# Starting the first row's score maxima beside the second row's input stage

## The chip, the cores and the metric

The kernel runs on one core of one Trainium2 chip. The metric is the device time of one execution in microseconds (us). The kernel before was timed three times: 1706.95, 1707.77 and 1711.70 us, so the median is 1707.77 us. A profile was taken of one further execution.

## The reference, cut to what matters

The input x has 16 rows (b = 0 to 15) of 512 tokens with 128 features. Six residual blocks follow each other. Each begins with a layer norm.

```
x = x + 0.5 * kan(norm(x))          # small two-layer net per feature ("kan" below)
x = x + attention(norm(x))          # 16 query heads, 4 key heads, head size 8, rope, causal softmax
x = x + 0.5 * kan(norm(x))
x = x + 0.5 * experts(norm(x))      # 8 experts, each takes its 128 best tokens of every row
x = x + recurrence(norm(x))
x = x + 0.5 * experts(norm(x))
```

Only the first two blocks matter for the change. In the attention block, the scores of a query with all keys up to it are turned into weights by a softmax: the largest score of each query and head is subtracted before the exponential. So for each row the kernel first finds the maxima of the scores and then computes the scores a second time, with the maxima taken off, for the exponential.

## The kernel before, in words

**Layout.** A row is one tile of 128 partitions x 4 x 128 numbers. The kernel treats the 16 rows one after another through a pipeline of stages, and the stages of different rows lie beside each other. All engine orders (TensorE, VectorE, ScalarE, GpSimd) are the order in which the program emits the instructions; each engine works strictly through its own list. The SP engine, which issues the DMAs, also works through one list.

**Stages of a row.** `stage_in` (L582) runs `kan` (L329) and then `attn_in` (L415). `attn_in` normalizes the row, makes queries, keys and values with matrix products (L424, L430, L436, L444), applies rope on VectorE (L425, L431, L437, L445), and splits queries and keys into three bf16 parts on ScalarE and GpSimd (`parts`, L393, eight GpSimd operations with the rope sums at L440 and L463). `spread` (L408) then writes the parts to DRAM, and the packed keys `kp` (three DMAs, L476) and packed queries `qp` (four DMAs, one for each key head r, L484) are read back. There are NKP = 3 buffers of packed keys, so row b uses the buffer of row b - 3, and NQP = 10 buffers of packed queries.

`maxima` (L597) finds the row's score maxima in 44 steps, 11 for each of the four key heads: a step is a score product on TensorE (L611, with a causal mask added by L607 where a bank holds several heads) and one reduction on VectorE (L616 or L621). Two PSUM banks take turns, so TensorE can be at most two steps ahead of VectorE. After each half, `max_rows` (L625) turns the maxima into rows and sends them by DMA (L649, L651) into the packed queries.

`weights` (L657) computes the scores again in 44 steps: product on TensorE (L669), exponential on ScalarE (L672), mask on GpSimd (L674). It sets `taken[0]` to the number of key heads that have been emitted so far, over all rows. `outputs` (L680) multiplies by the values, and `stage_out` (L718) closes the attention, runs the second `kan` and the gate of the experts.

**The order is a matter of turns.** Everything is a Python generator; a *turn* (`turn`, L1098) emits what was put off (`flush`), gives one step to every urgent and every side generator and refills a budget for each engine. The main loop (L1127) goes over b from -1 to 15. A pass lasts TURNS = 44 turns, and in each turn one step of `weights(b)` and one step of `maxima(b + 1)` are emitted. The pass b = -1 has only the maxima of row 0, and the pass b = 0 is the first with weights. From b = 0 on the side generators are held to the engine budgets (`paced`). `forward` (L576) runs the `kan` of later rows ahead as long as `filling` is set, which is until the pass b = 0 begins.

**The start.** The pass b = -1 begins only when `finish(first, second)` (L1124) has run turns until the input stages of rows 0 and 1 are both completely emitted. Followed through the program's own counters, this gives the following turns for the kernel before:

| emitted | turn |
|---|---|
| row 0: DMAs of `kp` and `qp` | 45 |
| row 1: `attn_in` begins / its DMAs of `kp` and `qp` | 49 / 70 |
| pass b = -1 begins (maxima of row 0) | 71 |
| row 2: `attn_in` begins / its DMAs | 72 / 93 |
| `kan` of row 3 | 67 to 98 |
| `kan` of row 4 | 98 to 129 |
| pass b = 0 begins (weights of row 0, maxima of row 1) | 115 |
| row 3: `attn_in` begins / its DMAs | 138 / 165 |
| pass b = 1 begins | 159 |
| pass b = 2 begins | 203 |

At the end of the passes b = 0 and later `finish(ins[b + 2])` (L1157) makes sure that the row needed two passes later is through.

Of the kernel before, what the change touches and what calls it, by code (L numbers as in the profile page):

```python
# [25 lines left out]
NR = 4  # L26
# [3 lines left out]
NKP = 3  # L30
# [16 lines left out]
def tile_macaron(  # L47
# [10 lines left out]
    B = x_in.shape[0]  # L58
# [40 lines left out]
    with ExitStack() as ph:  # L99
# [90 lines left out]
        def packed(b):  # L190
            return [QP[(NR * b + r) % NQP] for r in range(NR)], KP[b % NKP]
# [17 lines left out]
        def step(g):  # L209
            return g is not None and next(g, g) is not g  # L210
# [10 lines left out]
        def need(**work):  # L221
            while paced[0] and any(w > room[e] for e, w in work.items()):
                yield
            for e, w in work.items():
                room[e] -= w

        def take(**work):

            for e, w in work.items():
                room[e] -= w  # L230

        def refill():
            now[0] += 1
            room.update(MOST)
# [8 lines left out]
        def bank(shape, dtype, name, work=0.0):  # L243


            while held[0] == 2 or (paced[0] and work > room["pe"]):
                yield
            room["pe"] -= work
            held[0] += 1
            return mm.tile(shape, dtype, name=name, tag="mm")  # L250

        def freed():
            held[0] -= 1
# [154 lines left out]
        def spread(part, heads, name):  # L408

            scr = tc.dram_tile([3, HD, heads, S], BF16, name=name)  # L410
            for i in range(3):
                nc.sync.dma_start(out=scr[i].rearrange("d h t -> h d t"), in_=part[:, i, :])
            return scr

        def attn_in(b, st):  # L415
            _, xT = yield from norm(x[b])
            ka = w1p.tile([KR, S], F32, name="rope_ka")
            kb = w1p.tile([KR, S], F32, name="rope_kb")
            ta = w1p.tile([P, S], F32, name="rope_a")
            tb = w1p.tile([P, S], F32, name="rope_b")  # L420
            qpart = w1p.tile([P, 3, S], BF16, name="qpart")
            kpart = w1p.tile([KR, 3, S], BF16, name="kpart")
            pa = yield from bank([P, S], F32, "ps_pa", 0.9)
            nc.tensor.matmul(pa, lhsT=wq.rearrange("k h d -> k (h d)"), rhs=xT, start=True, stop=True)  # L424
            later.append(lambda: nc.vector.tensor_mul(ta, pa, rope[:, 0, :]))  # L425
            yield
            take(dve=0.7)
            freed()
            pb = yield from bank([P, S], F32, "ps_pb", 0.9)
            nc.tensor.matmul(pb, lhsT=wqr.rearrange("k h d -> k (h d)"), rhs=xT, start=True, stop=True)  # L430
            later.append(lambda: nc.vector.tensor_mul(tb, pb, rope[:, 1, :]))  # L431
            yield
            take(dve=0.7)
            freed()
            pk = yield from bank([2 * KR, S], F32, "ps_pk", 0.9)
            nc.tensor.matmul(pk, lhsT=wk.rearrange("k w h d -> k (w h d)"), rhs=xT, start=True, stop=True)  # L436
            later.append(lambda: nc.vector.tensor_mul(ka, pk[0:KR, :], rope[0:KR, 0, :]))  # L437
            yield
            yield from need(pool=1.25)
            nc.gpsimd.tensor_tensor(ta, ta, tb, ALU.add)  # L440
            take(dve=0.7)
            pv = yield from bank([P, NT, KR], F32, "ps_v", 0.9)
            for c in range(NT):
                nc.tensor.matmul(pv[:, c, :], lhsT=xT[:, bass.ts(c, P)], rhs=wv, start=True, stop=True)  # L444
            later.append(lambda: nc.vector.tensor_mul(kb, pk[KR : 2 * KR, :], rope[KR : 2 * KR, 1, :]))  # L445
            yield
            take(dve=0.7)
            freed()
            qp_steps = parts(ta, qpart, nc.scalar.copy, act=0.6)
            step(qp_steps)  # L450

            va = vap.tile([P, NT, NR, 32], F32, name="va")
            nc.gpsimd.memset(va[:, :, :, HD:32], 0.0)
            nc.gpsimd.memset(va[:, :, :, HD : HD + 1], 1.0)
            later.append(lambda: nc.vector.tensor_copy(va[:, :, :, 0:HD], pv.rearrange("p c (r d) -> p c r d", d=HD)))
            yield
            take(dve=0.3)
            freed()
            st["va"] = va

            def keys():
                yield from need(pool=1.25)
                nc.gpsimd.tensor_tensor(ka, ka, kb, ALU.add)  # L463
                yield
                yield
                yield
                yield from parts(ka, kpart, nc.scalar.copy, act=0.6)

            yield from together(qp_steps, keys())
            qp, kp = packed(b)  # L470

            ks = spread(kpart, NR, f"ks{b}")
            qs = spread(qpart, NH, f"qs{b}")
            N = 3 * HD
            for j in range(3):
                nc.sync.dma_start(  # L476
                    out=kp[j * N : (j + 1) * N, :, :],
                    in_=ks[j].rearrange("d r t -> d (r t)").unsqueeze(0).to_broadcast([3, HD, NR * S]),
                )
            for r in range(NR):  # L480
                while taken[0] < NR * b + r - NQP + 1:
                    yield
                src = qs[:, :, r * NG : (r + 1) * NG, :].rearrange("i d h t -> (i d) (h t)")
                nc.sync.dma_start(out=qp[r][0 : 3 * N, :, :],  # L484
                                  in_=src.unsqueeze(0).to_broadcast([3, N, NG * S]))
            yield
# [95 lines left out]
        def stage_in(b, st):  # L582
            late = b in through
            yield from kan_in(b)
            for _ in range(LATE if late and b > 2 else 0):
                yield
            yield from attn_in(b, st)
# [164 lines left out]
        def routing(k, g):  # L752


            while scored[k] < (g + 1) * GB:
                yield
            N = GB * E
            sc3 = scores[g].rearrange("p c b e -> p (c b) e")
            mx = rtp.tile([P, NT * GB], F32, name="mx")
            probs = rtp.tile([P, NT, N], F32, name="probs")  # L760
            pr3 = probs.rearrange("p c (b e) -> p (c b) e", e=E)
# [13 lines left out]
            yield from rest(2)  # L775
            ps = yield from bank([N, NT, P], F32, "ps_p")
            for c in range(NT):
# [314 lines left out]
        taken = [0]  # L1092
        sts = [dict() for _ in range(B)]
# [4 lines left out]
        def turn():  # L1098
            flush()
            urgent[:] = [g for g in urgent if step(g)]  # L1100
            sides[:] = [g for g in sides if step(g)]
            refill()

        def finish(*gs):
            pace, paced[0] = paced[0], False
            while any(g in sides for g in gs):
                turn()
            paced[0] = pace
# [4 lines left out]
        first = stage_in(0, sts[0])  # L1113
# [7 lines left out]
        second = stage_in(1, sts[1])  # L1121
        sides.append(second)
        sides.append(forward())
        finish(first, second)  # L1124
        ins = {2: stage_in(2, sts[2])}
        sides.append(ins[2])
        for b in range(-1, B):  # L1127
            if b == 2:
                sides.append(folded())
                sides.extend(routing(k, g) for k in range(2) for g in range(NG2))  # L1130
            if b == B - 1:
                expert_weights()
                sides.append(fetch())
            filling[0], paced[0] = b < 0, b >= 0
            wts = weights(b, sts[b]) if b >= 0 else None
            mxs = maxima(b + 1, sts[b + 1]) if b + 1 < B else None
            if b >= 0:
                sts[b]["y"] = w2p.tile([P, NT, NR, NG, HD], F32, name="y")
                sts[b]["out"] = []
            for i in range(TURNS):  # L1140
                flush()
                step(wts)
                step(mxs)
                if b >= 0 and i and i % len(BANKS) == 0:
                    urgent.append(outputs(b, sts[b], i // len(BANKS) - 1))
                if b > 0 and i == OUT:
                    sides.append(stage_out(b - 1, sts[b - 1]))
                if b + 4 < B and i == IN:
                    ins[b + 4] = stage_in(b + 4, sts[b + 4])
                    sides.append(ins[b + 4])  # L1150
                turn()
            flush()
            step(mxs)
            if b >= 0:
                urgent.append(outputs(b, sts[b], NR - 1))
            if b >= 0 and b + 2 < B:
                finish(ins[b + 2])  # L1157
        hurry[0], paced[0] = True, False
        while len(sts[B - 1]["out"]) < NR:
# [64 lines left out]
```

## Time and profile before

| quantity | value |
|---|---|
| median of three runs | 1707.77 us |
| the profiled execution's own time | 1714.79 us |
| its span, first to last instruction | 1713.1 us |
| mean granted TensorE clock | 0.965 |
| busy share: TensorE, VectorE, ScalarE, GpSimd | 93%, 66%, 58%, 59% |
| first VectorE reduction of row 0's maxima | 76.3 us |
| first exponential of rows 0, 1, 2, 3 and 4 | 121.3, 164.7, 214.4, 272.2, 326.0 us |

The profile gives, for one execution, when each engine was busy. A pass of the main loop can be read from the trace by the first exponential of each row: row 0's marks the start of the pass b = 0, row 1's that of b = 1, and so on. In the middle of the kernel a pass lasts 53.9 us. "PEclk" and "granted clock" are the share of the full TensorE clock that the chip granted: 1.00 is full, 0.50 half.

### The profile page before, as it was taken

Reading aid. Unit: us, or ns where it says so; the run is one execution under the profiler, and the core shown is the slowest. Engines: PE = TensorE matmul, PEld = TensorE weight load, DVE = VectorE, ACT = ScalarE, POOL = GpSimd, SP = SyncE. Lnnn points to the kernel's source line nnn. Section 1 sums busy time; section 2 is a strip of 40 time slices with the busy share of each in tenths; the row PEclk is TensorE's granted clock in tenths of the full one; section 3 lists DMA queues with packets and bytes.
Section 4 is the critical chain, followed back from the end, with each engine's and each line's share of the span. In section 5 each row is a group of like instructions: output and inputs, shape, how many; then the busy total and the mean of one; then the engine's idle time right before and its main releaser. Section 6 shows DMA issues by size and latency. Waiting matters only on the chain. (4 is left out here: it accounts for less than half of the span.)

```text
span 1713.1 us, 35403 instructions
## 1 busy us (share of the span) xinstructions
PE 1593.3 (93%) x12943; PEld 1106.1 (65%) x12943; DVE 1124.4 (66%) x3606; ACT 1000.5 (58%) x2000; POOL 1019.0 (59%) x1486
## 2 busy tenths in 40 slices
PE   5689999999999999999998898999999999999997
PEld 2234444445454444445444598888888789999997
DVE  6578778888898888898984239444377344762222
ACT  3336767788777876777666663444452334445443
POOL 2635547556665656556636666666672867657773
PEclk9769989999999999999999899999998999999999
DMA  4210111011111111111122122332331323323333
GB/s 121 67 60 27 55 48 41 32 43 52 56 33 39 42 55 34 37 42 55 55 72 59 33 55 58 64 62 62 68 63 39 65 58 75 65 52 72 74 75 49
DMA packets 103093, 94.87 MB, mean 55 GB/s; under 512 B 13197, under 2 KB 91478, under 8 KB 102678
## 3 DMA queue, kind: packets, MB, share of 16 engines
q1 hardware_dynamic: 76060, 67.65, 13.0%
q0 software_dynamic: 26048, 24.93, 9.1%
q8 instruction: 102, 1.67, 0.4%
q14 instruction: 73, 0.60, 0.1%
q10 hardware_dynamic: 810, 0.02, 0.0%
HBM read 59.00 MB, written 37.49 MB: 56 GB/s over the span
## 5 line engine op out<-in xcount | busy, mean ns | idle before, releaser
L674 POOL TENSOR_SCALAR_AFFINE_SELECT pt<-pt 128x128 f32<-128x128 f32 (+2 forms) x704 | 251.7, 364 | 333.2 <-ACT pt L672 328.2
L672 ACT ACTIVATE pt<-ps_st 128x512 f32<-128x512 f32 (+1 forms) x704 | 378.6, 563 | 100.6 <-PE ps_st L669 94.7
L616 DVE CUSTOM_DVE_ANT_0 below<-ps_sc,causal 128x512 bf16<-128x512 f32 (+1 forms) x512 | 315.0, 615 | 81.1 <-PE ps_sc L611 65.7
L933 ACT ACTIVATE mo<-ps_h 128x512 f32<-128x512 f32 x256 | 152.8, 597 | 272.2 <-PE ps_h L931 270.3
L857 POOL DMA_INDIRECT xg<-xnd,tokI x256 | 249.5, 975 | 82.7 <-issue 38.7
L931 PE MATMUL ps_h<-xin,mw 128*128 128x128 f32 x2048 | 281.1, 281 | 0.0
L669 PE MATMUL ps_st<-qp,kp 99*128 99x512 bf16 (+3 forms) x1024 | 258.2, 304 | 21.5 <-ACT pt L672 20.7
L946 PE MATMUL ps_y<-mw,mo 128*128 128x128 f32 x2048 | 275.3, 278 | 2.0 <-DVE mo L955 2.0
L611 PE MATMUL ps_sc<-kp,qp 72*128 72x512 bf16 (+3 forms) x1024 | 261.2, 307 | 11.5 <-DVE maxs L616 6.6
L931 PEld LDWEIGHTS ps_h<-xin,mw 128*128 128x128 f32 x2048 | 252.5, 194 | 6.3 <-issue 3.7
L978 POOL DMA_INDIRECT sum<-ye,tokI x124 | 200.3, 1616 | 94.4 <-issue 38.1
L946 PEld LDWEIGHTS ps_y<-mw,mo 128*128 128x128 f32 x2048 | 252.6, 194 | 4.5 <-DVE mo L955 3.3
L669 PEld LDWEIGHTS <-kp 99*128 99x128 bf16 x1024 | 95.2, 101 | 182.2 <-issue 164.8
L371 ACT ACTIVATE kan_h<-kan_s,rbias,kw 128x512 f32<-128x512 f32 x256 | 205.6, 812 | 4.1 <-PE ps_kg L365 4.1
L692 PE MATMUL ps_av<-pt,va 128*32 128x512 f32 (+3 forms) x2048 | 165.7, 442 | 0.0
L621 DVE TENSOR_REDUCE maxs<-ps_sc 128x2 f32<-128x512 f32 (+1 forms) x192 | 130.1, 685 | 38.4 <-PE ps_sc L611 37.9
L611 PEld LDWEIGHTS <-qp 72*128 72x128 bf16 x1024 | 96.6, 100 | 80.3 <-issue 57.7
L952 DVE TENSOR_TENSOR mo<-mo 128x128 bf16<-128x128 f32 x132 | 38.2, 289 | 131.7 <-ACT mo L937 131.5
L964 PE MATMUL acc<-mo 128*128 128x128 bf16 x1584 | 113.0, 220 | 6.2 <-DVE mo L952 6.1
L692 PEld LDWEIGHTS ps_av<-pt,va 128*32 128x32 f32 x2048 | 53.7, 109 | 94.9 <-issue 43.7
L964 PEld LDWEIGHTS <-mo 128*128 128x128 bf16 x1584 | 99.6, 99 | 23.7 <-issue 22.4
L294 POOL TENSOR_TENSOR ln_rstd<-ln_rstd,mhalf 128x4 f32<-128x4 f32 x96 | 101.7, 1059 | 8.0
(197 smaller groups left out, 2376.9 us busy)
## 6 DMA issues: line engine op xcount, KB each, us to landing
qp<-qs SPq DMA_DIRECT2D x64, 288.0 KB
xnd<-kan_x SPq DMA_DIRECT2D x32, 256.0 KB
sum<-x SPq DMA_DIRECT2D x31, 256.0 KB
qs<-qpart SPq DMA_DIRECT2D x48, 128.0 KB
kp<-ks SPq DMA_DIRECT2D x48, 96.0 KB
x<-in_L_attn_x_dram SPq DMA_DIRECT2D x16, 256.0 KB
mw<-in_L_ffn_w_dram SPq DMA_DIRECT2D x16, 256.0 KB
xg<-xnd,tokI POOLq DMA_INDIRECT x256
```

The source lines that it names most:

```text
L371: nc.scalar.activation(h, sk[half], AF.Relu, bias=rbias[:, half, v : v + 1], scale=kw1[:, half, v : v + 1])
L611: nc.tensor.matmul(v[:, u, 0:n], lhsT=qp[r][0 : 9 * HD, g, bass.ts(c, P)], rhs=kp[0 : 9 * HD, r, 0:n], start=alone, stop=(u == len(gs) - 1 ...
L616: nc.vector.tensor_tensor_reduce(below[:, 0:n], v[:, 0, 0:n], causal[:, S - n : S], 1.0, LOWEST, ALU.add, ALU.max, accum_out=maxs[:, c, h ...
L669: nc.tensor.matmul(v[:, u, 0:n], lhsT=kp[ROWS, r, bass.ts(c, P)], rhs=qp[r][ROWS, g, c * P : S], start=True, stop=True)
L672: nc.scalar.activation(o, v[:, :, 0:n], AF.Exp, scale=HD ** -0.5)
L674: nc.gpsimd.affine_select(out=dg, in_=dg, compare_op=ALU.is_ge, fill=0.0, base=0, pattern=[[0, len(gs)], [1, P]], channel_multiplier=-1)
L692: nc.tensor.matmul(po[32 * g : 32 * g + 32, c * P : S], lhsT=va[:, c, r, :], rhs=pt[:, g, OFF[c] : OFF[c] + n], start=(c == 0), stop=(c == ...
L857: nc.gpsimd.indirect_dma_start(out=xgs[i // E % 2][:, i % E, :], out_offset=None, in_=xnd[b], in_offset=bass.IndirectOffsetOnAxis(ap=tokI[ ...
L931: nc.tensor.matmul(pst[:, f, :], lhsT=mw1[e][:, bass.ts(f, P)], rhs=xins[i // E % 2][:, i % E, :], start=True, stop=True)
L946: nc.tensor.matmul(py, lhsT=hs[u][:, f, :], rhs=mw2[e][:, f, :], start=(f == 0), stop=(f == NF - 1))
L964: nc.tensor.matmul(acc[:, c, :], lhsT=sels[u][:, bass.ts(c, P)], rhs=yes[u][:, w, :], start=(e == 0 and c == 0 and w == 0), stop=(e == las ...
L978: nc.gpsimd.indirect_dma_start(out=sums[k, b], out_offset=bass.IndirectOffsetOnAxis(ap=tokI[g][:, n : n + 1], axis=0), in_=ye[:, b % 2 * ( ...
```

## The change

The input stage of row 1 is no longer waited for. After row 0's input stage has been emitted, nine more turns are run, and then the pass b = -1 begins, while row 1's input stage still runs as a side generator. Row 2's input stage is started there too, as before. Row 1's stage now has to be through by the end of the pass b = -1, for which `finish(ins[b + 2])` is also called at b = -1. Since row 3's input stage can now come early enough to reach its key DMAs before row 0's weights are emitted, `attn_in` waits, before its three key DMAs, until all weights of the row three in front (the last user of the same key buffer) have been emitted.

```diff
@@ attn_in
             ks = spread(kpart, NR, f"ks{b}")
             qs = spread(qpart, NH, f"qs{b}")
             N = 3 * HD
+            while taken[0] < NR * (b - NKP + 1):
+                yield
             for j in range(3):
                 nc.sync.dma_start(
                     out=kp[j * N : (j + 1) * N, :, :],
@@ main part
         second = stage_in(1, sts[1])
         sides.append(second)
         sides.append(forward())
-        finish(first, second)
-        ins = {2: stage_in(2, sts[2])}
+        finish(first)
+
+        for _ in range(9):
+            turn()
+        ins = {1: second, 2: stage_in(2, sts[2])}
         sides.append(ins[2])
         for b in range(-1, B):
             if b == 2:
@@ end of a pass
             step(mxs)
             if b >= 0:
                 urgent.append(outputs(b, sts[b], NR - 1))
-            if b >= 0 and b + 2 < B:
+            if b + 2 < B:
                 finish(ins[b + 2])
```

The same turns for the changed kernel: row 1's `attn_in` still begins at 49 and its DMAs still go out at 70; the pass b = -1 begins at 55; row 2's `attn_in` at 67 and its DMAs at 88; the `kan` of rows 3 and 4 stay at 67 to 98 and 98 to 129; the pass b = 0 begins at 99; row 3's `attn_in` at 98, with its parts written at 126 and its `kp` and `qp` DMAs held until 143; the pass b = 1 begins at 143 and the pass b = 2 at 187. From the pass b = 2 on the instructions of every engine stand in the same order as before, 16 turns earlier: of about 9,410 rows of TensorE's order the last 8,939 are the same.

## The prediction

> **What bounds the kernel now.** I read the page's slices first, since the change touches only the first tenth of the kernel:
>
> ```profile
> PE   5689999999999999999998898999999999999997
> DVE  6578778888898888898984239444377344762222
> PEclk9769989999999999999999899999998999999999
> ```
>
> A slice is 43 us. TensorE (PE) is full from slice 4 on, but 50%, 60% and 80% busy in the first three, and its clock is 0.7 and 0.6 in slices 2 and 3. Time can only be had here. From the pass b = 2 on the order of every engine is unchanged, so the whole effect is how much earlier row 2's first exponential comes; it is at 214.4 us now, and what follows (1713.1 - 214.4 = 1498.7) I keep.
>
> The second view is a table of busy time by stretches. Columns: stretch, its length, then busy us and instruction count of PE, weight loads, DVE, ACT, POOL, then clock, DMA share, GB/s.
>
> ```profile
> 57.00:60.20 3.20, 2.92 (x13) 0.96 (x13) 0.13 (x1) 0.59 (x1) 0.00 (x0) 0.50 0.19 72
> 60.20:65.00 4.80, 4.80 (x15) 1.85 (x11) 1.80 (x3) 2.22 (x3) 0.65 (x1) 0.71 0.19 79
> 65.00:68.30 3.30, 2.52 (x21) 1.57 (x21) 1.24 (x3) 1.21 (x2) 3.05 (x5) 1.00 0.32 111
> 68.30:76.30 8.00, 0.63 (x4) 0.12 (x3) 3.32 (x11) 0.62 (x1) 7.26 (x8) 0.60 0.30 104
> 76.30:83.50 7.20, 6.33 (x13) 2.88 (x14) 5.80 (x22) 1.17 (x2) 2.50 (x3) 0.50 0.16 49
> 83.50:93.70 10.20, 8.92 (x46) 3.86 (x46) 9.21 (x23) 6.83 (x11) 4.85 (x6) 1.00 0.28 100
> 93.70:121.60 27.90, 24.49 (x82) 10.60 (x81) 20.40 (x62) 6.78 (x11) 7.47 (x8) 0.50 0.17 62
> 121.60:165.00 43.40, 40.96 (x300) 19.41 (x299) 34.84 (x107) 28.45 (x55) 19.31 (x49) 0.97 0.07 21
> 165.00:214.40 49.40, 45.46 (x347) 22.28 (x346) 39.78 (x127) 33.83 (x64) 31.71 (x64) 1.00 0.17 55
> ```
>
> From 68.3 to 76.3 nearly nothing runs but POOL. From 76.3 to 121.6 is the pass b = -1: PE is busy 88%, but mostly at half clock, and DVE 78%. The passes b = 0 and 1 are bound by PE (94% and 92% busy at full clock). The hole is seen in the timeline of PE (start, us):
>
> ```profile
> 58.30 1.94 PE L365 MATMUL ps_kg<-kan_h,w2d 128*32 128x512 f32 x8
> 60.16 2.08 PE L424 MATMUL ps_pa<-kan_xT,wq 128*128 128x512 f32 x2
> ...
> 68.33 0.60 PE L611 MATMUL ps_sc<-kp,qp 72*128 72x512 bf16 x2
> 76.50 1.09 PE L318 MATMUL ps_t<-ident,kan_x 128*128 128x128 f32 x4 [7.58 <-DVE kan_x L308]
> ```
>
> The first two score products are done at 68.9; then all wait for DVE, which has row 2's and 3's norm (L308) ahead of the first reduction and waits for `ln_rstd` from POOL, which works off row 1's eight parts operations first. The maxima start at 76.3.
>
> **The change, part by part.**
>
> *When can the maxima start?* In the new order PE has three L611 products straight after the L365 group that ends at 60.2, ahead of row 1's L424. They need row 0's packed keys and the first packed queries, issued here:
>
> ```profile
> 54.52 2.35 SPq L476 DMA_DIRECT2D kp<-ks  x3
> 56.98 2.87 SPq L484 DMA_DIRECT2D qp<-qs  x4
> ```
>
> By the trace's semaphore events the keys land at 58.2, 59.7 and 61.2, the four queries at 65.0, 68.8, 72.6 and 77.0. The engines' share of 0.19 is 3 of 16, so these four share three DMA engines, 3.8 us each. Thus PE stands still from 60.2 to 65.0 and the first reduction can start at 65.7, not at turn 55's own place near 60. Queued behind the wait are row 1's four products L424 to L444, which slip by about 6.6 us (60.2 to 66.8), and with them POOL's chain for row 1 (64.4 to about 71.7) and row 1's DMAs. The start is 76.3 - 65.7 = 10.6 us earlier. Later heads are no limit: 11 steps take over 7 us, a packed query 3.8.
>
> *Turns 55 to 72.* Sixteen reductions stand on DVE ahead of the two L308 copies. Their prices:
>
> ```profile
> L616 DVE CUSTOM_DVE_ANT_0 below<-ps_sc,causal 128x512 bf16<-128x512 f32 x256 | 174.3, 681 | 33.0 <-PE ps_sc L611 26.4
> L616 DVE CUSTOM_DVE_ANT_0 below<-ps_sc,causal 128x384 bf16<-128x384 f32 x256 | 140.7, 550 | 48.1 <-PE ps_sc L611 39.4
> L621 DVE TENSOR_REDUCE maxs<-ps_sc 128x2 f32<-128x512 f32 x128 | 86.8, 684 | 16.6 <-PE ps_sc L611 16.5
> ```
>
> With 0.08 us for reading out each L616: 8 x 0.76 + 5 x 0.63 + 3 x 0.69 = 11.3 us. Between them: row 1's rope 4 x 0.69 + 0.29 = 3.05, one x addition 0.69, two norms' statistics 2 x (0.87 + 0.36) = 2.5. Sum 17.5 us, so 83.2. POOL's `ln_rstd` for both copies: the chain begins at 71.7 (PE's L430 at half clock), 9.2 us up to its second key part (as 64.4 to 73.4 now), then 2 x 1.3: 83.5. So DVE and POOL arrive together; with the two copies (1.5) and some waiting for half-clock products I take 85.5. The 8 us hole is gone because DVE has reductions to do in it.
>
> *Turns 72 to 99.* Now, the same two copies pass DVE at turn 77 and 81.8 us, and pass b = 0 begins at turn 115, 121.6: 38 turns in 39.8 us, 1.047 a turn. After the change the 27 turns hold the same work but for row 4's first `kan` products. Bounds: by DVE alone, 27 x 0.70 + rope 3.1 + maxima rows 1.5 + x 0.7 + statistics 2.5 = 26.7 us; by PE, at full clock and with 0.24 us for a turn's score products (0.22 between the starts of two of 512 columns): the 38 turns hold 9.1 + one L318 0.6 + two L338 2.0 + row 2's four products 4.1 + L365 2.1 + L386 1.05 + row 4's first products 2.7 = 21.6; the 27 turns hold 6.5 + two L318 1.3 + 2.0 + 4.1 + 2.1 + 1.05 = 17.0, so 39.8 x 17.0 / 21.6 = 31.3. I take the pitch of the row itself, 27 x 1.047 = 28.3: pass b = 0 begins at 113.8 instead of 121.6, 7.8 us earlier.
>
> *What comes back in pass b = 0.* Row 4's first products, L318 0.66 and L338 2 x 1.0 (full-clock durations), now stand in this pass, which is bound by PE: +2.7. Row 3's `attn_in` lies inside it both times. It begins with 2.9 us of half clock now (up to 124.5); with denser work this may end sooner, -0.8. So 43.4 + 1.9 = 45.3. Pass b = 1 keeps stage_out, row 4's `attn_in` and all offsets; only row 3's last key operations on POOL leave it: I keep 49.7 - 0.3.
>
> *The new wait in `attn_in`.* It is a wait in turns, not on an engine. It holds only row 3 (turns 126 to 143); for the others the condition is met already. Row 3's keys and queries then go out 44 turns ahead of their maxima (187), now 38 (165 to 203): nothing, between 0 and 0 since 22 us of DMA fit. `finish(ins[1])` finds row 1 through at turn 70: no turns.
>
> *DMAs moved on SP.* Row 1's packed tensors land about 6 us later, last near 106 (100.4 now), needed from 113.8. Row 0's maxima rows (L649, L651) stand behind row 2's first four part writes and one key load; I place their landing near 110. If that cover were gone, each us late would cost one us of PE.
>
> *A rule against it.* The trace shows clock 0.50 after PE's idle stretches, and half clock for 27.9 us with PE 24.49 us busy. The Trainium skill ("TensorE: Matmul & The Clock Gate", Part 1) says that an idle window of about 3.4 us halves the clock and that one busy window of 3.4 us restores it. By the rule the new idle stretch of 4.8 us costs the clock until about 70 and then the dense products of rows 1 and 2 restore it: turns 72 to 99 run at DVE's 26.7, a gain of 7.5 us. By the row, 88% busy is not enough to restore it, and PE's 31.3 is nearer: gain 2.9. The measurement decides that the rule is too kind; I stay between, at 28.3.
>
> **Sum.** 113.8 + 45.3 + 49.4 = 208.5 against 214.4: 5.9 us less. The profiled execution would take 1714.79 - 5.9 = 1708.9, the median, 7.0 below it, 1707.77 - 5.9 = 1701.9.
>
> **Rivals.**
> *PE keeps the account (within 0.3%).* For: passes -1 to 1 carry the same products, PE was 88 to 94% busy in them, and idle time bought early is paid in pass b = 0. Against: the hole of 8 us is real. At 31.3 us the gain is 2.9: 1704.9. Chance 0.37.
> *Half clock throughout (slower).* Place: 65 to pass b = 0. If the reductions leave gaps between products that keep PE at 0.50, the 17.0 us become 34.0, at 88% busy 38.6; with 2 us more before turn 72, pass b = 0 begins at 126.1 and the end is 126.1 - 113.8 - 5.9 = 6.4 later: 1714.2. It decides from a pitch of 1.27 us a turn on (85.5 + 27 x 1.27 = 119.7). For: 27.9 us of it now. Against: more dense f32 products lie in these turns. Chance 0.10.
> *It does not do what it says.* If row 0's queries landed later than 72 or row 1's DMAs after 113.8, turns would be earlier only on paper. The landings speak against it; it is in the 0.37.
>
> **Numbers.** Forecast 1701.9, faster: 0.53; same 0.37; slower 0.10. A measurement of this kernel can tell about 0.3% (5.1 us) from no change. The likeliest case alone reaches from 1699 to 1702.6, by DVE's bound and a quicker pass b = 0. The range takes in the second rival and run-to-run spread: 1697.5 to 1707.8.
>
> **What would show it.** Right: PE idle from about 60 to 65 with the queries' DMA named, first reduction near 65.7, no 8 us hole at 68, row 0's first exponential near 114, row 1's near 159, row 2's near 208.5. Wrong: a clock of 0.50 through to row 0's exponential, PE waiting for `qp` at the start of pass b = 0, a pass b = 0 over 47 us, or a different time after row 2.

## The result and the profile after

| | before | after |
|---|---|---|
| median | 1709.61 us (20 runs) | 1713.54 us (20 runs) |
| ratio, 95% interval | | 1.0021, 1.0011 to 1.0031 |
| profiled execution, span | 1713.1 us | 1709.4 us |
| first reduction of row 0's maxima | 76.3 us | 64.6 us |
| first exponential of rows 0, 1, 2 | 121.3, 164.7, 214.4 us | 119.9, 169.4, 217.8 us |

The change makes the kernel 0.2% slower, some 4 us, where 5.9 us less was forecast. The profiled execution of after happens to be a short one: behind row 2's first exponential it needs 1709.4 - 217.8 = 1491.6 us, before's needed 1498.7, with the same order of instructions in both. The clock records explain such differences: behind the mark TensorE stood at half clock for 37 us in after's execution and for 66 us in before's. So one span can't judge a change of 4 us. The many runs can: +3.9 us by the medians. Row 2's mark has the same sign, +3.4 us, but the next pass takes part of it back: pass b = 2, the same instructions in both, meets 10.2 us of half clock in before and lasts 57.7 us, and in after 3.4 and 55.2 us, so that row 3's first exponential is only 0.9 us later (273.0 against 272.2).

Three chips were used for the experiments: chip 5 for e1 to e8, chip 6 for e9 to e11, chip 13 for e12 to e14. On chip 5 all runs take 4.5% longer and scatter by 2 to 3%, so there I read the marks first and the ratio second. The ratios take in only runs within 1.5% of the fastest of their kernel (12 of the 22 of e5), and the traces of e2 and e6 are of slower executions than that.

The page's slices, whose lines of before stand in the prediction:

```profile
PE   5689999999999998999998898999999999999997
DVE  6577879888888888898984239544378343762222
PEclk9769999999999999999999899999999999999999
```

At this scale nothing has changed: the first three slices are as empty as before. The stretches tell more (columns as in the prediction: stretch, length, busy us and count of PE, weight loads, DVE, ACT, POOL, then clock, DMA share, GB/s):

```profile
59.20:64.00 4.80, 0.05 (x1) 0.06 (x2) 0.00 (x0) 2.22 (x3) 0.00 (x0) 0.50 0.19 79
64.00:71.50 7.50, 7.14 (x11) 2.09 (x11) 4.55 (x12) 0.00 (x0) 0.92 (x1) 0.50 0.19 79
71.50:81.80 10.30, 6.59 (x44) 3.51 (x44) 9.57 (x35) 1.80 (x3) 8.53 (x11) 1.00 0.23 73
81.80:92.00 10.20, 9.02 (x24) 4.09 (x24) 6.60 (x15) 1.76 (x3) 2.98 (x4) 0.50 0.20 72
92.00:98.80 6.80, 4.77 (x23) 2.27 (x21) 5.68 (x11) 4.04 (x6) 3.71 (x5) 1.00 0.27 98
98.80:119.90 21.10, 17.52 (x65) 6.48 (x65) 14.77 (x42) 4.14 (x6) 7.35 (x7) 0.51 0.18 61
119.90:133.00 13.10, 11.22 (x37) 5.43 (x35) 9.61 (x39) 6.29 (x12) 5.95 (x13) 0.61 0.06 23
133.00:169.40 36.40, 34.79 (x274) 17.23 (x273) 27.48 (x77) 27.09 (x51) 22.48 (x46) 1.00 0.13 40
169.40:217.80 48.40, 45.45 (x348) 22.25 (x347) 38.55 (x127) 33.74 (x64) 25.83 (x57) 1.00 0.14 43
```

The hole at 68 to 76 is gone. In its place PE and DVE both stand still from 59.2 to 64.0, and then half clock alternates with stretches in which DVE is the busy one. The pass b = -1 now takes 119.9 - 64.6 = 55.3 us (45.0 before), the pass b = 0 takes 49.5 (43.4) and the pass b = 1 48.4 (49.7). The timeline of PE shows the new stall (start, us; in brackets the idle time before it and who ended it; the lines are two further down than before):

```profile
57.25 1.94 PE L365 MATMUL ps_kg<-kan_h,w2d 128*32 128x512 f32 x8
63.95 1.03 PE L613 MATMUL ps_sc<-kp,qp 72*128 72x512 bf16 x2 [4.76 <-DMA qp<-qs]
65.34 0.58 PE L613 MATMUL ps_sc<-kp,qp 72*128 72x512 bf16 x1 [0.36 <-DVE maxs L618]
65.73 1.91 PE L424 MATMUL ps_pa<-kan_xT,wq 128*128 128x512 f32 x2
```

Row 1's first product L424 starts at 65.7 (60.2 before) and takes 1.9 us for its two instructions. The three products that follow take 1.9, 1.8 and 1.0 us.

### The profile page after: what moved, and what is told of

The parts are those of the page before. It is cut to its first block, busy times and chain, and to the rows that moved or that the text cites. A ratio compares the mean times of both kernels' runs of the same rounds, so it can differ in the third digit from the quotient of the medians.

```text
span 1709.4 us, 35405 instructions
## 1 busy us (share of the span) xinstructions
PE 1585.3 (93%) x12943; PEld 1097.8 (64%) x12943; DVE 1125.3 (66%) x3606; ACT 1000.3 (59%) x2000; POOL 1021.2 (60%) x1486
## 5 line engine op out<-in xcount | busy, mean ns | idle before, releaser
L671 PE MATMUL ps_st<-qp,kp 99*128 99x512 bf16 (+3 forms) x1024 | 258.7, 305 | 21.3 <-ACT pt L674 20.8
L694 PEld LDWEIGHTS ps_av<-pt,va 128*32 128x32 f32 x2048 | 53.7, 109 | 94.4 <-issue 44.1
```

Of the source, the lines that this page charges most:

```text
L671: nc.tensor.matmul(v[:, u, 0:n], lhsT=kp[ROWS, r, bass.ts(c, P)], rhs=qp[r][ROWS, g, c * P : S], start=True, stop=True)
L694: nc.tensor.matmul(po[32 * g : 32 * g + 32, c * P : S], lhsT=va[:, c, r, :], rhs=pt[:, g, OFF[c] : OFF[c] + n], start=(c == 0), stop=(c == ...
```

## The experiments

After the result I had two theories. *Half clock*: the score products wait one by one for VectorE, this keeps PE at 0.50, and the pass takes longer for it. *Wait in front of row 1*: the first score product waits for its packed queries, and all that stands behind it on PE, row 1's four products and through them row 1's rope and its GpSimd chain, is held up and then done inside the pass. The rival to both was *account*: PE has no slack, its products were only moved.

The marks of all runs, each from one trace, in us. "Half" is the half clock by the clock records from the first reduction to row 1's first exponential.

| run | first reduction | row 0 | row 1 | row 2 | half | ratio to before, 95% interval |
|---|---|---|---|---|---|---|
| before | 76.3 | 121.3 | 164.7 | 214.4 | 37.9 | |
| e10, before again | 73.9 | 117.7 | 161.5 | 211.2 | 24.0 | (one run) |
| after | 64.6 | 119.9 | 169.4 | 217.8 | 47.9 | 1.0021, 1.0011 to 1.0031 |
| e8, after again (chip 5) | 64.8 | 118.8 | 166.6 | 215.0 | 39.6 | 1.0043, 1.0014 to 1.0073 |
| e1, after filled (chip 5) | 64.5 | 114.4 | 162.9 | 211.3 | 16.8 | 0.9962, 0.9933 to 0.9990 |
| e2, before filled (chip 5) | 73.9 | 116.6 | 158.5 | 208.2 | 7.0 | 0.9967, 0.9939 to 0.9995 |
| e3, 15 turns (chip 5) | 64.0 | 112.2 | 159.0 | 208.1 | 34.1 | 1.0001, 0.9973 to 1.0030 |
| e4, row 3 late (chip 5) | 65.6 | 120.7 | 168.4 | 217.8 | 44.2 | 1.0025, 0.9997 to 1.0054 |
| e5, 15 turns, filled (chip 5) | 64.2 | 112.2 | 158.9 | 208.1 | 10.2 | 0.9913, 0.9880 to 0.9947 |
| e6, query in three (chip 5) | 64.0 | 118.0 | 165.8 | 214.2 | 39.6 | 1.0031, 1.0002 to 1.0060 |
| e7, 20 turns (chip 5) | 67.4 | 119.3 | 164.3 | 214.0 | 41.0 | 0.9997, 0.9972 to 1.0022 |
| e9, wait filled | 65.4 | 117.7 | 167.2 | 215.6 | 41.0 | 1.0021, 1.0007 to 1.0035 |
| e11, 15 turns, filled, three | 64.3 | 110.4 | 155.8 | 204.9 | 13.7 | 1.0000, 0.9987 to 1.0013 |
| e12, before with the wait alone | 80.0 | 123.9 | 169.2 | 218.9 | 34.7 | 1.0033, 1.0018 to 1.0047 |
| e13, 15 turns again | 64.4 | 112.7 | 159.4 | 208.5 | 34.1 | 0.9987, 0.9979 to 0.9996 |
| e14, 15 turns, three | 64.5 | 112.8 | 159.5 | 208.7 | 34.1 | 0.9976, 0.9965 to 0.9988 |

The start of an execution moves all marks by up to 1.5 us (the first product of L365 starts at 19.3 to 20.8 us), and the same program's marks differ by some 3 us from trace to trace (before: 214.4 and 211.2; after: 217.8 and 215.0). Row 2's marks are not carried to the end in full: the pass b = 2, the same work in every run, lasts 53.7, 55.2 to 55.4 or 57.7 to 58.2 us as it meets none, 3.4 or 10.2 us of half clock.

**e1 and e2: extra products in the pass b = -1, changed kernel and kernel before.** Nobody reads these products; the outputs do not depend on them.

```diff
+        idle = stp.tile([P, S], F32, name="ps_idle", tag="ps_st")
+        def warm(n):
+            for _ in range(n):
+                nc.tensor.matmul(idle, lhsT=identb, rhs=causal, start=True, stop=True)
...
                 step(mxs)
+                if b < 0:
+                    warm(1)
```

Expected, e1: 

> The changed kernel, with one extra 128x512 bf16 product of two constants on TensorE in each of the 44 turns of the pass b = -1; nobody reads it. It adds 44 x 0.21 us = 9 us of TensorE work at full clock. Theory 'half clock' (the change loses because TensorE stands at 0.50 for most of the stretch from row 0's first score product to row 1's pass): the extra work keeps the clock at 1.00, the pass b = -1 is bound by VectorE, row 0's first exponential comes near 111 us instead of 119.9, row 1's 45 to 46 us later, and the kernel is 8 to 12 us faster than the changed one, faster than the one before too. Theory 'account' (TensorE's products are only moved and it has no slack): the extra 9 us is added, row 0's first exponential comes at 125 to 128 us and the kernel is 5 to 9 us slower than the changed one.

Expected, e2: 

> The kernel before, with the same extra product in each of its 44 turns of the pass b = -1. Theory 'half clock': the pass takes 38 to 41 us instead of 45, row 0's first exponential comes at 114 to 117 us instead of 121.3, the kernel is 4 to 7 us faster than before. Theory 'account': 5 to 9 us slower. If this one gains as much as the filled changed kernel does, the clock is a matter of the pass and not of the change.

Measured: 9 us of work more on PE and yet row 0's mark 4.5 to 5.6 us earlier than in the two traces of after, and 0.4% less time than before. "Account" is out for the pass b = -1. The two stretches behind the two L308 copies, changed kernel first, then e1:

```profile
85.30:119.90 34.60, 28.81 (x102) 11.96 (x103) 23.75 (x61) 9.70 (x15) 11.05 (x11) 0.61 0.20 71
```

```profile
85.20:114.40 29.20, 24.93 (x127) 11.44 (x128) 23.21 (x61) 9.38 (x15) 11.07 (x11) 0.94 0.22 79
```

The same 27 turns and the same 61 instructions on DVE take 34.6 us at a mean clock of 0.61 and 29.2 at 0.94. The kernel before gains as well (e2), so the half clock belongs to the pass and not to the change. But e1 is by row 2 no earlier than the kernel before in its second trace (211.3 and 211.2), and its gain in row 0's mark, some 5 us, fell short of the 9 expected (111 instead of 119.9). With the clock raised in both, the changed kernel is still 3.1 us behind at row 2 (211.3 and 208.2), nearly the 3.4 and 3.8 us by which after is behind before without the extra products. So another cost remained, and it is the one that belongs to the change.

**e3, e13 and e7: 15 turns instead of nine, in e7 20.**

```diff
-        for _ in range(9):
+        for _ in range(15):
             turn()
```

Expected, e3: 

> The changed kernel with 15 turns instead of nine between row 0's input stage and the pass b = -1: row 1's four products stand ahead of the first score product on TensorE, so that the wait of 4.8 us for the packed queries goes; row 3's input stage falls back into its late place (turn 128, inside pass b = 0). Theory 'half clock', with the wait as what sets it off: row 1's products run at full clock again, the kernel is 3 to 5 us faster than the changed one, equal to before or better. Theory 'account': within 1.5 us of the changed kernel.

Expected, e13: 

> The 15-turn kernel again: is it faster than the kernel before in whole runs as it is at row 2's mark (208.1 against 214.4 and 211.2)? Theory 'wait in front of row 1': 0.2 to 0.4% faster than before. Rival: what is won by row 2 is lost in the passes behind it to half clock, ratio within 0.1% of 1.

Expected, e7: 

> The changed kernel with 20 turns instead of nine. The wait for the queries is gone as with 15, and the five turns more let row 3's first norm come closer to the first reductions on VectorE. Theory 'wait': row 2's exponential within 2 us of the 15-turn kernel's 208.1, since what matters is only that row 1's products stand first. Theory 'account': it moves back towards the kernel before, 211 to 213 us.

Measured: with 15 turns the first reduction is as early as with nine (64.0 and 64.4), and all later marks are 6 to 10 us earlier. PE's timeline of e13:

```profile
57.21 1.94 PE L365 MATMUL ps_kg<-kan_h,w2d 128*32 128x512 f32 x8
59.08 2.03 PE L424 MATMUL ps_pa<-kan_xT,wq 128*128 128x512 f32 x2
60.94 1.02 PE L430 MATMUL ps_pb<-kan_xT,wqr 128*128 128x512 f32 x2
61.89 1.07 PE L436 MATMUL ps_pk<-kan_xT,wk 128*64 128x512 f32 x2
62.90 1.08 PE L444 MATMUL ps_v<-wv,kan_xT 128*128 128x32 f32 x8
63.81 0.60 PE L613 MATMUL ps_sc<-kp,qp 72*128 72x512 bf16 x2
```

Row 1's products fill exactly the time in which the queries are on their way; nothing waits, and the score products start when they did anyway. In whole runs this version is a little faster than before in e13, 0.9987, between the 0.1% of the rival and the 0.2 to 0.4% that I expected; e3's 1.0001 on chip 5 can't tell. With 20 turns most of the marks' gain is given up again (row 2 at 214.0, not within the 2 us of 208.1 that I expected): the first reduction comes at 67.4, and the pass has 34.1 us of half clock. So it is not enough that row 1's products stand first. What else the five turns cost stays open, and the whole runs don't separate 20 turns from 15 (0.9997 and 1.0001).

**e4: only row 3's input stage late again.**

```diff
-            late = b in through
+            late = b in through or b == 3
```

Expected: 

> The changed kernel, with only row 3's input stage put back to its late start (28 turns after its first block, so at turn 126 instead of 98), which takes it away from the norm of row 4 and out of the first turns of pass b = 0. Theory 'half clock' and theory 'account' both expect little here: pass b = 0 between 47 and 50 us as now (49.5), the kernel within 1.5 us of the changed one. If row 3's early stage is what costs, pass b = 0 falls to 45 us and the kernel is 3 to 4 us faster than the changed one.

Measured: pass b = 0 takes 47.7 us (49.5 and 47.8 in the traces of after), row 2's mark stays at 217.8. By these marks row 3's early stage, and with it the new wait in turns, is not what costs; the whole runs (1.0025 against e8's 1.0043 on the same chip) are too coarse to add to that. The 15-turn kernel has row 3 late too, so this run also says that this is not its merit.

**e5: 15 turns and the extra products.** The edits are those of e3 and e1.

Expected: 

> The changed kernel with 15 turns instead of nine and with the extra unread product in each turn of the pass b = -1. In the 15-turn kernel the pass b = -1 still had 27.8 us of half clock and took 48.2 us. Theory 'wait and clock' (row 1's products held behind the queries' DMA cost some 7 us of the pass, half clock the rest): row 0's first exponential comes at 106 to 109 us, row 2's at 202 to 205 us, and the kernel is 0.5 to 0.8% faster than before. Theory 'account': the fill costs its 9 us again, row 2's exponential at 213 us or later.

Measured: half clock falls from 34.1 to 10.2 us, and the marks do not move (112.2, 208.1). With row 1's products out of the way, DVE is the busiest engine of the pass:

```profile
64.20:110.00 45.80, 36.90 (x189) 17.25 (x192) 39.44 (x116) 11.62 (x18) 22.68 (x24) 0.96 0.24 85
110.00:112.20 2.20, 0.61 (x2) 0.25 (x2) 0.36 (x1) 0.05 (x1) 0.00 (x0) 0.88 0.19 71
```

DVE is busy 86% of the first stretch, and the 2 us behind it are a wait of 1.7 us for row 0's maxima rows, which are late on the DMA queue. The marks missed the expected 202 to 205; the ratio of 0.9913 is not borne out by the marks, which equal e3's, and it rests on the faster half of this run's scatter.

**e6: the first packed queries in three DMAs.**

```diff
+                if b == 0 and r == 0:
+                    for k in range(3):
+                        nc.sync.dma_start(out=qp[r][k * N : (k + 1) * N, :, :], in_=src)
+                    continue
```

Expected: 

> The changed kernel, nine turns, with the DMA of row 0's first packed queries cut into three of 24 x 3 = 72 lines of 4 KB each, which no longer share three DMA engines: the queries land about 3 us earlier and TensorE's wait of 4.8 us shrinks to 1 to 2 us, with nothing else moved. Theory 'wait': row 0's first reduction comes 3 us earlier and row 2's exponential 3 to 5 us earlier (213 to 215 us instead of 217.8). Theory 'clock alone': the gain of the start is lost in the pass, row 2's exponential between 216.5 and 218.5.

Measured: the wait only falls from 4.8 us (5.9 in e8) to 3.1 us.

```profile
PE ps_sc L617 <- DMA qp<-qs: 3.1, 1, 3.1
```

The three DMAs still end behind the three key DMAs. Row 0's and row 2's marks are both 0.8 us earlier than e8's, 2.3 if the later start of this execution is taken off, about what the wait lost. Row 2's 214.2 lies where theory 'wait' put it, but e8, without the edit, is at 215.0 and its whole runs are no different (1.0043 and 1.0031). It does not decide between the theories; the step was too small.

**e9: extra products in the wait and nowhere else.**

```diff
+        warm(14)
         for b in range(-1, B):
```

Expected: 

> The changed kernel with 14 unread 128x512 bf16 products ahead of the first score product, so that they lie in TensorE's wait of 4.8 us for the packed queries and in nothing else. If the idle stretch of the wait is what brings the half clock, row 1's four products run at full clock (1.0 us each instead of 1.9), the clock stays up for some 10 us after, and row 0's first exponential comes 3 to 5 us earlier (114 to 117 us). If the half clock comes from the pass itself, whose products wait one by one for VectorE, row 1's products gain at most 2 to 3 us and the pass falls back to 0.50: row 0's first exponential at 117 to 119.5 us.

Measured:

```profile
65.00:71.50 6.50, 5.64 (x26) 2.49 (x27) 5.75 (x16) 0.49 (x1) 1.74 (x3) 1.00 0.19 78
71.50:80.00 8.50, 4.79 (x33) 2.47 (x33) 8.12 (x33) 1.33 (x3) 7.73 (x9) 0.97 0.30 94
80.00:117.70 37.70, 30.94 (x109) 12.71 (x109) 26.91 (x66) 9.94 (x15) 13.98 (x15) 0.60 0.21 72
```

Row 1's products now run at full clock, but from 80 on the clock is as low as without (0.60), row 0's mark is 1.1 to 2.2 us earlier than after's (2.6 to 3.3 with the starts taken off), and in whole runs nothing is gained: 1.0021. The idle stretch as a cause of half clock is at most a small part of the cost.

**e10: before again.** Expected: 

> The kernel before once more, for a second trace of it: every theory expects the first reduction at 75 to 77 us, row 0's first exponential at 120 to 122 us and row 2's at 213 to 215.5 us. If these marks scatter by more than 2 us, the difference of 3.4 us between the two first traces means little.

Measured: 73.9, 117.7 and 211.2, some 3 us earlier than in the first trace, 1.4 us of it by the start. I had set 2 us as the limit, so single marks alone would not carry the sign of the change; two traces of each (at row 2 +3.4 and +3.8 us, at row 3 +0.9 and +3.5) and the runs do.

**e8: the changed kernel once more,** on chip 5, without an edit.

Expected: 

> The changed kernel itself once more, for its ratio on this chip and for how far the marks of the trace scatter: all theories expect row 0's first exponential at 119 to 121 us, row 2's at 217 to 219 us, and 0.1 to 0.3% slower than before.

Measured: 64.8, 118.8, 166.6 and 215.0, ratio 1.0043. The sign is that of the first result; row 2's mark is below the 217.8 of the other trace, by about as much as e10's is below before's. This is where the 3 us of scatter come from that the table is to be read with.

**e11 and e14: 15 turns, the query DMAs of rows 0 to 2 in three each, with and without the extra products.** Edits as in e6 (with `b <= 2`), e3 and e1.

Expected, e11: 

> The 15-turn kernel with the extra products, and the query DMAs of rows 0 to 2 cut into three each, so that they spread over more DMA engines. In the filled 15-turn kernel TensorE waited 1.7 us at the start of pass b = 0 for row 0's maxima rows, which queue behind those DMAs. Theory 'wait': this wait goes, row 0's first exponential comes 1 to 2 us earlier than 112.2 and row 2's at 206 to 207 us; the fastest of all. Rival: SP's eight more issues per row (0.7 us each) make the same DMAs late, row 0's first exponential stays at 112 us or later.

Expected, e14: 

> 15 turns, with the query DMAs of rows 0 to 2 in three each, without extra products: row 0's queries land earlier still and the maxima rows do not queue behind them. Theory 'wait in front of row 1': the wait was already gone with 15 turns, so row 0's first exponential is within 1.5 us of 112.2 (half clock in the pass as before), the ratio that of the 15-turn kernel within 0.1%.

Measured: e11 has the earliest marks of all (110.4 and 204.9, no wait for the maxima rows), yet its whole runs equal before's, 1.0000, and are not the fastest of all. e14 has e13's marks and 0.9976, so without the extra products the whole runs are, if anything, better. Why e11's gain of 6 to 10 us at row 2 does not reach the end stays open; the order behind the mark is the same. In its trace the gain is still there at row 3 (262.9, before 272.2 and 269.2), and what follows row 2 takes 1502.7 us with 70 us of half clock, the most outside chip 5.

**e12: the wait alone, put into the kernel before.** One unread score product is added; the pass b = -1 still begins at turn 71.

```diff
-        finish(first, second)
+        finish(first)
+        for _ in range(9):
+            turn()
+        idle = stp.tile([P, S], F32, name="ps_idle", tag="ps_st")
+        nc.tensor.matmul(idle, lhsT=QP[0][0 : 9 * HD, 0, 0:P], rhs=KP[0][0 : 9 * HD, 0, :], start=True, stop=True)
+        finish(second)
```

Expected: 

> The kernel before with one instruction added on TensorE: an unread score product of row 0, placed where the changed kernel has its first one (ahead of row 1's four products), so that TensorE waits for the packed queries there; everything else, the start of the pass b = -1 included, stays as before. Theory 'wait in front of row 1' (row 1's products and its GpSimd chain are held up and that is paid in full): row 0's first exponential 3.5 to 6 us later than before (121 to 126 us), the kernel 0.2 to 0.35% slower than before. Rival 'hidden' (the 8 us hole at 68 takes it up): within 1.5 us of before.

Measured: 1.0033. The timeline of PE:

```profile
63.44 0.61 PE L1128 MATMUL ps_idle<-kp,qp 72*128 72x512 bf16 x1 [5.25 <-DMA qp<-qs]
63.84 1.92 PE L424 MATMUL ps_pa<-kan_xT,wq 128*128 128x512 f32 x2
...
72.05 0.60 PE L611 MATMUL ps_sc<-kp,qp 72*128 72x512 bf16 x2
80.22 1.08 PE L318 MATMUL ps_t<-ident,kan_x 128*128 128x128 f32 x4 [7.58 <-DVE kan_x L308]
```

The hole of 7.58 us is there in full, only later: it does not swallow the wait. It is made by row 1's GpSimd chain, and the chain waits for the held-up products. The first reduction comes at 80.0 (76.3 and 73.9 before), row 0's mark at 123.9 (121.3 and 117.7), in an execution that starts 1.4 us earlier than before's first. One instruction in the wrong place of PE's list costs some 5.6 us (0.33% of 1710; by the interval 3 to 8).

## Why the prediction was wrong, point by point

*Only the stretch up to row 2 matters.* Right in the order, and near in time: +3.4 us at the mark, +3.9 us in the medians. But the pass b = 2 alone lasts 53.7 to 58.2 us with the same work, so that the nearness of the two numbers is in part luck. The tail's own variation in one execution (7 us) was larger than I allowed for when I took the span as a base.

*The maxima start 10.6 us earlier, and PE stands still for the queries.* Right: 64.6 against 76.3, of which 1 us is the start; a wait of 4.76 us with the queries' DMA named.

*Turns 55 to 72: DVE and POOL arrive together at 85.5.* Right: the two copies were through at 85.3.

*Turns 72 to 99, "I take the pitch of the row itself, 27 x 1.047 = 28.3".* Wrong, and the largest term: 34.6 us, 1.28 a turn. Of the 9.3 us between the forecast of 208.5 for row 2's mark and 217.8, 6.3 lie here and 4.2 in the pass b = 0; the pass b = 1 and the copies give 1.2 back. The stretch of before that the pitch was taken from:

```profile
81.80:121.60 39.80, 35.11 (x129) 14.94 (x129) 30.20 (x87) 13.90 (x22) 12.32 (x13) 0.63 0.20 72
```

Its clock was 0.63, and in after it was 0.61, so the clock does not make the difference between the two. The work of a turn does, for the greater part: PE was busy 35.11 us in 38 turns, 0.92 a turn, and is now busy 28.81 us in 27, 1.07 a turn. The side work of rows 2 and 3 does not shrink with the number of turns, so a pitch per turn could not be carried over. Scaled by PE's work it is 28.3 x 1.07 / 0.92 = 32.9, an estimate; the rest of the 34.6 is not explained. e1 took 29.2 us for the same turns at a clock of 0.94, so the pitch of before is reached here only at nearly full clock. With row 1's products in front (e13), the 33 turns behind the two copies took 36.5 us, 1.11 a turn. My rival "half clock throughout" had named 1.27 a turn as the point from which it decides; I gave it 0.10.

*"What comes back in pass b = 0", +1.9.* Wrong in size: 49.5 and 47.8 against 43.4 and, in e10, 43.8, on average +5.0. Half clock in it was 10.2 and 6.8 us against 3.1 and 4.1, which at half speed is (8.5 - 3.6) / 2 = 2.4 us; the products of row 4, 2.7 us, come to it. I had taken 0.8 us off for denser work; the half clock grew instead.

*The wait priced as a later start.* This was the step that failed in kind. I took the wait into the start (65.7) and into POOL's chain (71.7), and up to the two copies that came out. Behind them I charged nothing for it, although row 1's four products, 1.9 + 1.9 + 1.8 + 1.0 = 6.6 us, now lie inside the pass. e12 shows that the wait in this place costs some 5.6 us of the whole run even where the pass does not start early, and e3 and e13 that with row 1's products in front of it the same early start is kept and the marks move 6 to 10 us. e13's marks, 112.7, 159.4 and 208.5, are nearly those that I forecast for the changed kernel (113.8, 159.1 and 208.5); as the single terms differ, that agreement is in part luck, and of the 5.9 us forecast its whole runs show 2.2. How the loss divides between the wait and the denser turns is not shown; they overlap, since row 1's held-up work is part of what makes the pass dense.

*The rule.* The Trainium skill, "TensorE: Matmul & The Clock Gate", Part 1, would have one window of about 3.4 us of sustained work restore the clock. In after it came back at 71.5, when PE had been busy 7.14 of 7.50 us, and at 92.0, after 9.02 of 10.20 us. From 98.8 to 119.9 PE was busy 17.52 of 21.1 us at 0.51 and it did not; nor did it in before from 97.1 to 104.0, with PE busy 6.84 of 6.90 us by the records at 0.50. What decides is open. By the rule I would have been further off (26.7 for the turns 72 to 99); the between that I chose was too near to it.

*The new wait in `attn_in`, `finish(ins[1])`, the DMAs on SP.* Right as far as seen: PE waits for no DMA at the start of pass b = 0 in after, and e4 moves nothing.

## What to carry to other kernels

An engine that works through its list in order makes a wait cost what stands behind it, not what it waits for: before an early start is put into such a list, put in front of it what is ready and would otherwise be held up. Here six turns more kept the same start and took the wait away, while eleven more lost most of it again, so the place has to be tried. And a pitch per turn holds only for the work of those turns: when the same side work is packed into fewer turns, the pitch rises, here from 1.05 to 1.28 us at the same granted clock.

## What the runs showed of the hardware

- TensorE at half clock and 83 to 88% busy by the records did not get its clock back for 20 to 30 us (before: 24.49 of 27.90 us busy at 0.50). One unread 128x512 product per turn kept it at 0.94 (e1, the last 27 turns) and 0.96 (e5).
- More work on an engine can make its stretch faster: with the unread products the same 27 turns took 29.2 us instead of 34.6 (e1). Whether that pays in whole runs is not settled: e2 took 0.9967 (0.9939 to 0.9995) on chip 5, but the 15-turn kernel took 1.0000 with these products (e11) and 0.9976 without (e14).
- The same instructions behind row 2's mark took 1488 to 1503 us in the eight traces outside chip 5, mostly with the half clock met there (30 to 70 us).
